# Low halves of the output weights made on GpSimd instead of VectorE, in a two-layer gated cross-attention block

## The chip, the cores and the metric

The kernel runs on one NeuronCore of a Trainium2 chip. The metric is the device time of one execution in microseconds (us). The core has five instruction queues that run side by side and wait for each other by semaphores: TensorE (PE; its weight loads are listed apart as PEld), VectorE (DVE), ScalarE (ACT), GpSimd (POOL) and SyncE (SP), which here issues every DMA. Each engine takes its own queue strictly in order.

## The reference

The input `x` is (4, 512, 512), the context (4, 512, 256), all float32. Four sub-layers are added to `x` one after another, each behind a tanh gate:

```
x = x + tanh(g_xattn[0]) * mamba(context, layernorm(x))      # conv, selective scan over 512 steps, 16 states
x = x + tanh(g_ffn[0])   * bitnet(layernorm(x))              # ternary weights, 8-bit activations
x = x + tanh(g_xattn[1]) * attention(layernorm(x), context)  # 16 heads of 128, RMS-normed q and k
x = x + tanh(g_ffn[1])   * experts(layernorm(x))             # 4 experts, 512 wide
```

What the change touches is the last product of the attention:

```
out = einsum('bhqk,bkhd->bqhd', attn, v).reshape(B, Sq, H * D)
return out @ Wo                                              # Wo is (16 * 128, 512)
```

## The kernel before

**Two halves for one float32.** Matmuls run in float16. A float32 matrix `w` is scaled by a power of two `S` and kept as a high half `hi = fp16(w * S)` and a low half `lo = fp16(w * S - hi)`; a product then takes three matmuls (`mm3`, line 252). The helper `split` (lines 241 to 244) makes the halves: ScalarE writes `hi` (L243), VectorE writes `lo` in one instruction (L244, `w * S - hi`). Everything that is split goes through these two lines, so the profile shows them under many names: `qT`, `oT`, `hlwk`, `hlwq`, `hlwo` and others.

**Staging of the attention weights.** The 16 heads form four groups (hg 0 to 3). For each group, `attention_weights` takes Wk, Wq and Wo in turn (units named `wk0`, `wq0`, `wo0`, `wk1`, ...). `raw_load` (L265) brings 128x2048 float32 of raw weights to SBUF (for k half of that), `staging` (L276) squares its pieces of 128x512 on ScalarE (L289) to find `S` (a matmul with ones at L228, then a short chain on VectorE and GpSimd, L215 to L221), splits them piece by piece, and stores both halves to DRAM (L298). Four pieces make one unit of Wo. The attention of all four batches later reads these halves back head by head (`wk` L850, `wq` L916, `wo` L1021). The raw tile and the tile of halves both come from the pool `big`, which has three buffers; the next units and the ternary weights of the bitnet layer of batches 1 and up (`w`, loaded at L715) take the same three buffers. A unit must be finished before its buffers go to the next.

**Where this happens.** Group 0 is staged in the prologue. Groups 1 to 3 are staged as filler work during the attention of batch 0: at every softmax, `filler` advances the generator by four pieces. At the same time `layer0(1)` runs, first the scan of batch 1. So in this stretch three streams share the engines: the attention heads of batch 0, the scan of batch 1, and the staging.

**The scan.** For each of 16 states and each 128-channel tile t, one step (L646 to L664) loads a row of B and a row of C broadcast to all partitions (`bc` L646, `cc` L648, five buffers together), ScalarE makes `dA` in PSUM (L652), GpSimd makes `h = du * bc` (L186), VectorE scans `dA = dA * state + h` (L659 or L662) and multiplies by `cc` (L660; for every fourth step GpSimd does it, again under L186), and TensorE transposes and sums the result into `py` (L627). The tile of `h` comes from six buffers that are shared with other tiles.

**A head of the attention.** TensorE makes scores `ps`, VectorE their row maximum (L951), ScalarE the exponentials `pr` (L971), then the halves `hl` of the probabilities: for the heads up to number 8 of a batch GpSimd (L991) and ScalarE (L989) write the high ones and VectorE the low ones (L992); for the heads from 9 on in batches 0 to 2, one of each two is made on GpSimd alone, which first scales `pr` in place (L984) and then subtracts the high half (L986). `hl` goes through a transposing DMA (L994) to `pT`. After four heads, `project` (L1028) multiplies by Wo.

**The order of the instructions.** The program order is written out by hand (heads in a loop, the scan and the fillers between them at fixed rates), but the final order on each engine is set by a list scheduler that runs over the whole program with its own estimate of every instruction's length. An edit in one place can therefore change the order of instructions that the edit does not mention, on every engine.

Of the kernel before, what the change touches and what calls it, by code (L numbers as in the profile page):

```python
# [35 lines left out]
ALU = mybir.AluOpType  # L36
# [55 lines left out]
SC = 4  # L92
PT = 3
MT = 0
AV = 4
VB = 2
WB = 5
# [13 lines left out]
def flamingo_kernel(  # L111
# [8 lines left out]
    nc = tc.nc  # L120
# [29 lines left out]
    def bigt(shape, dtype, name):  # L150
        return big.tile(shape, dtype, tag="big", name=name)
# [7 lines left out]
    def sm(n, tag, name, bufs=4):  # L159
        return small.tile([P, n], F32, tag=tag, name=name, bufs=bufs)  # L160
# [63 lines left out]
    def total_pow2(tot, pool, name):  # L224

        n = tot.shape[1]
        ps = ap(f"frobps{name}") if pool is None else psum(pool, f"frobps{name}")
        nc.tensor.matmul(ps[:, :n], ones, tot, start=True, stop=True)  # L228
        if n == 1:
            return pow2(ps[:, 0:1], name)  # L230
        s = sm(1, "ftot", f"ftot{name}")
        nc.vector.tensor_reduce(s, ps[:, :n], AX.X, ALU.add)
        return pow2(s, name)
# [4 lines left out]
        nc.scalar.activation(junk, w, AF.Square, accum_out=tot)  # L238
        return total_pow2(tot, pool, name)

    def split(w, hi, lo, S):

        nc.scalar.activation(hi, w, AF.Copy, scale=S)  # L243
        nc.vector.scalar_tensor_tensor(lo, w, S, hi, ALU.mult, ALU.subtract)  # L244

    def mm3(ps, pairs, first=True, last=True):

# [11 lines left out]
    def raw_load(name, src, tile=bigt, parts=1):  # L259

        n, m = src.shape[1] // parts, src.shape[2]
        pieces = []
        for i in range(parts):
            raw = tile([P, n * m], F32, f"raw{name}{i}")
            nc.sync.dma_start(raw.rearrange("p (a b) -> p a b", a=n), src[:, i * n : (i + 1) * n])  # L265
            pieces += [raw[:, j : j + 512] for j in range(0, n * m, 512)]
        return pieces
# [8 lines left out]
    def staging(name, src, n, ps_pool, raw=None, store=True):  # L276

        if raw is None:
            raw = raw_load(name, src)
        w = 512 * len(raw)  # L280
        hl = bigt([P, 2 * w], F16, f"hl{name}")
        v = hl.rearrange("p (n s m) -> p n s m", n=n, s=2)
        pieces = [
            (r, *(v[:, j, s] if n > 1 else v[:, 0, s, j * 512 : (j + 1) * 512] for s in range(2)))
            for j, r in enumerate(raw)
        ]
        tot = sm(4, "stot", f"stot{name}", 2)
        for j, (r, hi, lo) in enumerate(pieces):
            nc.scalar.activation(hi, r, AF.Square, accum_out=tot[:, j : j + 1])  # L289
            yield  # L290
        S = total_pow2(tot[:, : len(pieces)], ps_pool, name)
        for r, hi, lo in pieces:
            split(r, hi, lo, S[:, 1:2])
            yield
        if not store:
            return None, S, hl
        d = dram.tile([P, 2 * w], F16, name=f"d{name}")
        nc.sync.dma_start(d, hl)  # L298
        return d, S, hl

    def attention_weights(hgs, ps_pool):

        units = [(hg, w) for hg in hgs for w in "kqo"]

        def load(hg, w):
            cols = slice(hg * 512, (hg + 1) * 512)
            return raw_load(f"w{w}{hg}", {
                "k": Wk[:, cols].rearrange("(k p) c -> p k c", p=P),
                "q": Wq[hg],
                "o": Wo[cols, :].rearrange("(h p) f -> p h f", p=P),  # L310
            }[w])

        kept = {"k": (wk_d, Sk), "q": (wq_d, Sq), "o": (wo_d, So)}
        raws = [load(*units[0])]
        for j, (hg, w) in enumerate(units):
            raws += [load(*u) for u in units[j + 1 : j + 2]]
            d, S, _ = yield from staging(f"w{w}{hg}", None, 1 if w == "k" else HG, ps_pool, raws[j])
            kept[w][0].append(d)
            kept[w][1].append(S)
            if w == "q":  # L320

                c = const.tile([P, 1], F32, name=f"ceq{hg}")
                nc.vector.tensor_scalar(c, S[:, 1:2], XS * QS * (HD * EPS) ** 0.5, None, ALU.mult)
                nc.vector.tensor_tensor(c, c, c, ALU.mult)
                nc.vector.tensor_tensor(c, c, gfac, ALU.mult)
                ceq.append(c)
# [4 lines left out]
    def values_of(b, hg, wv, ps_tile, v_tile):  # L331

        for c in range(T):
            rows = slice(c * P, (c + 1) * P)
            ps = ps_tile(f"pw{b}{hg}{c}")
            mm3(ps, [(cT[b][:, 0, k, rows], cT[b][:, 1, k, rows], wv[:, 0, k], wv[:, 1, k]) for k in range(2)])
            v = v_tile([P, 2, 512], F16, f"v{b}{hg}{c}")
            split(ps, v[:, 0], v[:, 1], QS)
            yield v

    def first_values(pool, ps_tile):


        for hg in range(NG):
            raw = bigt([P, 2, 512], F32, f"rawv{hg}")
            nc.sync.dma_start(raw, Wv[:, hg * 512 : (hg + 1) * 512].rearrange("(k p) c -> p k c", p=P))
            wv = pool.tile([P, 2, 2, 512], F16, tag="wv", name=f"wv{hg}", bufs=2)
            S = frobenius(raw, wv[:, 0], psv, f"wv{hg}")
            split(raw, wv[:, 0], wv[:, 1], S[:, 1:2])
            Sv.append(S)  # L350
            wv_d.append(dram.tile([P, 2048], F16, name=f"dwv{hg}"))
            nc.sync.dma_start(wv_d[hg], wv.rearrange("p s k c -> p (s k c)"))
            for b in range(PRE):
                for c, v in enumerate(
                    values_of(b, hg, wv, ps_tile, lambda s, d, n: pool.tile(s, d, tag="v", name=f"o{n}", bufs=VB))
                ):
                    nc.sync.dma_start(v_d[b][hg][:, c, :], v.rearrange("p s c -> p (s c)"))
                    yield
# [456 lines left out]
    def split_normed(xr, stats, hl, cols, name, tag="q", xn_tag="v"):  # L815


        xn = normed(xr, stats, name, xn_tag)
        xs = midt([P, 2, L], F16, f"xs{name}", tag)
        (nc.vector.tensor_copy if name[0] in XSD else nc.scalar.copy)(xs[:, 0], xn)  # L820
        nc.gpsimd.tensor_tensor(xs[:, 1], xn, xs[:, 0], ALU.subtract)
        nc.sync.dma_start_transpose(
            hl[:, :, :, cols].rearrange("p s k r -> p (s k) r"), xs.rearrange("p s f -> p (s f)")
        )

    def attention(b):
# [70 lines left out]
        def values(hg):  # L897
            def v_tile(shape, dtype, name):
                return at.tile(shape, dtype, tag="v", name=name, bufs=AV)

# [191 lines left out]
    def stage_expert(t, i):  # L1092

        j = 3 * t + i
        if j == 0:
            expert_raw(0)
        expert_raw(j + 1)
        e_d[t, i], e_S[t, i], hl = yield from staging(f"e{t}{i}", None, 1, pss, e_raw.pop(j), t < T - 1)
        hl = hl.rearrange("p (s k c) -> p s k c", s=2, k=T)
        if t == T - 1:  # L1100
            kept.append((hl[:, 0], hl[:, 1]))
        return hl[:, 0], hl[:, 1]
# [68 lines left out]
    def last_experts(pool, places):  # L1171
# [12 lines left out]
        for t in (T - 1, *range(T - 1)):  # L1184
            xTs[t] = pool.tile([P, 2, T, P], F16, tag="v", name=f"lxT{t}", bufs=AV)
            split_normed(x_sb[b][:, t, :], estats[b][t], xTs[t], slice(0, P), f"l{t}", "q")
# [22 lines left out]
    with tc.tile_pool(name="pro", bufs=1) as pro, tc.tile_pool(name="psp", bufs=4, space=PSUM) as psp:  # L1209
# [8 lines left out]

        if MT:
            wider["t"] = pro, MT  # L1220

# [79 lines left out]
    for i in range(-2, n):  # L1301
# [14 lines left out]
        w = steps[i // NH](i % NH, 2) if i >= 0 else iter(())  # L1316
# [98 lines left out]
```

## Time and profile before

| | |
|---|---|
| median of 3 runs | 2021.76 us (2015.58 to 2025.78) |
| the profiled execution | 2021.89 us |
| its span, first to last instruction | 2020.1 us |
| instructions | 27201 |
| mean granted TensorE clock | 0.879 |

The profile is one execution. For each engine it gives the busy time of every group of instructions (line, engine, operation, output <- inputs, shape), the mean length of one in ns, and the idle time just before them with what ended it ("who waited for whom"). A view by stretches gives the busy time of each engine between two moments, which tells what limits that stretch. A timeline lists the instructions in order of time, like ones merged. Busy times over a stretch of many engines don't add up: the stretch lasts as long as the engine or the chain that binds it.

### The profile page before, as it was taken

To read this page: it belongs to the slowest core of one execution; us is meant where nothing else is said; L and a number is where in the kernel's file an instruction comes from. 1 tells how busy PE (TensorE), PEld (TensorE's weight loads), DVE (VectorE), ACT (ScalarE), POOL (GpSimd) and SP (SyncE) were. 2 spreads that over 40 slices of the span, in tenths; PEclk is the share of its full clock that TensorE was granted. 3 is DMA by queue.
4 is the path that set the end of the run, shared out by engine and by line. 5 is a ranking of instruction groups with operands and counts; after the bars stand their busy time and mean duration, and the time that the engine had idled before them with its cause. 6 is when DMAs were issued, how large, how long until landed. Compare 5 with 4: busy or idle time off the path is not lost. (4 is left out here: it accounts for less than half of the span.)

```text
span 2020.1 us, 27201 instructions
## 1 busy us (share of the span) xinstructions
PE 1634.6 (81%) x8366; PEld 899.8 (45%) x8366; DVE 1541.3 (76%) x2893; ACT 1333.7 (66%) x3123; POOL 941.3 (47%) x931
## 2 busy tenths in 40 slices
PE   4364698657789987778999878798999879798888
PEld 1343233344444444455444554454444445455456
DVE  5899776999998778799886984999764565654664
ACT  6787656756666876475658665666565775857673
POOL 1886311785754269385414783675133441413211
PEclk8555798767789998989999899898999889898999
DMA  7454557778775587766435887676445686767655
GB/s 269 171 166 136 161 156 229 183 223 218 219 207 130 129 216 176 210 165 164 99 87 148 192 201 190 157 183 142 96 84 131 131 212 172 205 163 181 185 138 152
DMA packets 516322, 342.50 MB, mean 170 GB/s; under 512 B 425800, under 2 KB 427976, under 8 KB 510032
## 3 DMA queue, kind: packets, MB, share of 16 engines
q1 hardware_dynamic: 516176, 340.77, 64.9%
q8 instruction: 65, 1.06, 0.2%
q14 instruction: 81, 0.66, 0.1%
HBM read 193.10 MB, written 44.30 MB: 118 GB/s over the span
## 5 line engine op out<-in xcount | busy, mean ns | idle before, releaser
L186 POOL TENSOR_TENSOR h<-u,bc 128x512 f32<-128x512 f32 x256 | 338.2, 1341 | 86.4 <-DMA bc<-bd 43.7
L627 PE MATMUL py<-ident,h 128*128 128x128 f32 x1024 | 196.4, 337 | 123.9 <-DVE h L660 95.4
L652 ACT ACTIVATE dA<-delta,A 128x512 f32<-128x512 f32 x256 | 172.4, 685 | 140.5 <-DVE h L660 105.1
L252 PE MATMUL ps<-kT,qT 128*128 128x512 f16 x768 | 213.2, 399 | 50.1 <-ACT pr L971 34.4
L252 PE MATMUL pav<-pT,v 128*128 128x256 f16 x1536 | 215.6, 296 | 42.9 <-DMA pT<-hl 19.3
L659 DVE TENSOR_TENSOR_SCAN dA<-dA,h 128x512 f32<-128x512 f32 x200 | 240.7, 1217 | 11.4 <-POOL h L186 6.6
L627 PEld LDWEIGHTS py<-ident,h 128*128 128x128 f32 x1024 | 164.3, 213 | 166.7 <-DVE h L660 122.8
L951 DVE TENSOR_REDUCE nmx<-ps 128x1 f32<-128x512 f32 x256 | 172.4, 680 | 69.1 <-PE ps L252 68.8
L252 PE MATMUL pq<-axnT,wq 128*128 128x512 f16 x768 | 206.2, 423 | 19.9 <-DVE ksq L880 7.8
L992 DVE SCALAR_TENSOR_TENSOR hl<-pr,den,hl 128x512 f16<-128x512 f32 x214 | 193.7, 923 | 32.6 <-ACT hl L989 18.3
L971 ACT ACTIVATE pr<-ps,nmx,rqs 128x512 f32<-128x512 f32 x256 | 197.7, 775 | 14.2 <-DVE hl L992 10.1
L252 PEld LDWEIGHTS <-v 128*128 128x128 f16 x1536 | 161.5, 106 | 99.6 <-issue 33.8
L252 PE MATMUL pwo<-wo,oT 128*128 128x512 f16 x768 | 178.7, 383 | 9.0 <-DVE oT L244 5.5
L991 POOL TENSOR_SCALAR hl<-pr,den 128x512 f16<-128x512 f32 x86 | 63.6, 740 | 237.9 <-issue 104.6
L252 PEld LDWEIGHTS <-wq 128*128 128x128 f16 x768 | 83.1, 109 | 130.1 <-issue 64.6
L183 POOL TENSOR_TENSOR rqs<-ssq,mhalf 128x4 f32<-128x4 f32 x64 | 68.7, 1073 | 148.7 <-ACT ssq L940 140.9
L660 DVE TENSOR_TENSOR h<-dA,cc 128x512 f32<-128x512 f32 x200 | 134.3, 679 | 4.4 <-DMA cc<-bd 0.7
L252 PEld LDWEIGHTS <-qT 128*128 128x128 f16 x768 | 76.2, 102 | 137.0 <-issue 65.2
L252 PEld LDWEIGHTS <-cT 128*128 128x128 f16 x768 | 79.0, 105 | 113.3 <-issue 45.0
L252 PEld LDWEIGHTS <-oT 128*128 128x128 f16 x768 | 74.7, 99 | 99.8 <-DVE oT L244 8.4
L989 ACT ACTIVATE hl<-pr,den 128x512 f16<-128x512 f32 x128 | 91.8, 717 | 36.4 <-DVE den L978 30.0
L252 PE MATMUL pk<-wk,cT 128*128 128x512 f16 x384 | 106.4, 420 | 11.3 <-ACT ssq L940 6.2
(387 smaller groups left out, 3481.5 us busy)
## 6 DMA issues: line engine op xcount, KB each, us to landing
bc<-bd SPq DMA_DIRECT2D x112, 256.0 KB, 4.2
cc<-bd SPq DMA_DIRECT2D x112, 256.0 KB, 3.9
wq<-dwq SPq DMA_DIRECT2D x64, 256.0 KB, 4.4
wo<-dwo SPq DMA_DIRECT2D x64, 256.0 KB, 3.5
w<-w3d SPq DMA_DIRECT2D x12, 1024.0 KB, 7.0
de<-hle SPq DMA_DIRECT2D x9, 1024.0 KB, 5.5
lw<-de SPq DMA_DIRECT2D x18, 512.0 KB, 4.9
wk<-dwk SPq DMA_DIRECT2D x16, 512.0 KB, 3.5
```

The source lines that it names most:

```text
L183: nc.gpsimd.tensor_tensor(res, arg, mhalf[:, : arg.shape[1]], ALU.pow)
L186: nc.gpsimd.tensor_tensor(out, a, b, ALU.mult)
L252: nc.tensor.matmul(ps, l, r, start=first and i == 0, stop=last and i == n - 1)
L627: nc.tensor.matmul(ys[g // gs][:, g % gs, t, :], src[:, g::T], ident, is_transpose=True, start=first and t == 0 and g % gs == 0, stop=last ...
L652: last = nc.scalar.activation(dA, delta[t0 + t], AF.Exp, scale=A[:, t0 + t, n : n + 1])
L659: nc.vector.tensor_tensor_scan(dA, dA, h, 0.0, ALU.mult, ALU.add)
L660: nc.vector.tensor_tensor(h, dA, cc, ALU.mult)
L951: nc.vector.tensor_reduce(nmx[:, c : c + 1], ps, AX.X, ALU.max, negate=True)
L971: mark[0] = nc.scalar.activation(pr, scs[c], AF.Exp, bias=nmx[:, one], scale=rqs[:, one], accum_out=den[:, c - c0 : c - c0 + 1],).ins
L989: nc.scalar.activation(hl[:, c, 0], prs[c], AF.Copy, scale=den[:, one])
L991: nc.gpsimd.tensor_scalar(hl[:, c, 0], prs[c], den[:, one], 1.0, ALU.mult, ALU.mult)
L992: nc.vector.scalar_tensor_tensor(hl[:, c, 1], prs[c], den[:, one], hl[:, c, 0], ALU.mult, ALU.subtract)
```

## The change

For the units `wo1`, `wo2` and `wo3`, `split` no longer makes the low half on VectorE with one instruction. GpSimd makes it with two: the first scales the raw piece in place (`w = w * S`), the second subtracts the high half (`lo = w - hi`). The scaling overwrites the raw piece, so it has to wait until ScalarE has read it for `hi`. The three units have 12 pieces of 128x512 together. `wo0` and everything else that is split stays as it was. The line numbers of the changed kernel are higher by 1 from line 95, and by 5 behind `split`.

```diff
+STAGE_POOL = ("wo1", "wo2", "wo3")
...
-    def split(w, hi, lo, S):
+    def split(w, hi, lo, S, by_pool=False):
 
         nc.scalar.activation(hi, w, AF.Copy, scale=S)
-        nc.vector.scalar_tensor_tensor(lo, w, S, hi, ALU.mult, ALU.subtract)
+        if by_pool:
+            nc.gpsimd.tensor_scalar(w, w, S, 1.0, ALU.mult, ALU.mult)
+            nc.gpsimd.tensor_tensor(lo, w, hi, ALU.subtract)
+        else:
+            nc.vector.scalar_tensor_tensor(lo, w, S, hi, ALU.mult, ALU.subtract)
...
         for r, hi, lo in pieces:
-            split(r, hi, lo, S[:, 1:2])
+            split(r, hi, lo, S[:, 1:2], name in STAGE_POOL)
```

## Prediction

> **What bounds the kernel now.** I read the page first. Over the whole span no engine is full, so the average says little about a change that lives in one stretch:
>
> ```profile
> PE 1634.6 (81%) x8366; PEld 899.8 (45%) x8366; DVE 1541.3 (76%) x2893; ACT 1333.7 (66%) x3123; POOL 941.3 (47%) x931
> ```
>
> The view by tile says where the change lives: the instructions that write `hlwo` run from 218 to 592 us, four for `wo0` (kept) and twelve for `wo1` to `wo3`.
>
> ```profile
> L244 DVE SCALAR_TENSOR_TENSOR hlwo<-rawwo,Swo,hlwo x16: 734/750/1748, 230.6 to 592.3; 128x512 f16<-128x512 f32 x16
> ```
>
> The columns are min/median/max in ns. The wide maximum matters below. So I asked for the busy time by stretches around it (us in the stretch, then PE, PEld, DVE, ACT, POOL):
>
> ```profile
> 400.00:450.00 50.00, 31.49 (x149) 22.65 (x150) 48.74 (x66) 29.98 (x76) 38.31 (x32) 0.66 0.78 212
> 450.00:500.00 50.00, 33.44 (x173) 21.37 (x173) 46.13 (x75) 31.67 (x67) 29.39 (x25) 0.76 0.84 232
> 500.00:550.00 50.00, 37.84 (x185) 23.45 (x183) 46.84 (x71) 30.53 (x77) 35.59 (x30) 0.81 0.68 207
> 550.00:600.00 50.00, 40.40 (x227) 25.04 (x226) 47.45 (x95) 38.69 (x104) 28.00 (x28) 0.88 0.79 199
> 600.00:650.00 50.00, 49.23 (x244) 22.44 (x241) 42.09 (x118) 31.27 (x84) 21.36 (x33) 1.00 0.67 166
> ```
>
> From 400 to 600 us VectorE is busy for 92 to 97% and everything else has air; from 600 us TensorE takes over (98%). So twelve instructions are taken off the engine that binds. The timeline shows what one unit costs today:
>
> ```profile
> 422.39 4.48 DVE L244 SCALAR_TENSOR_TENSOR hlwo<-rawwo,Swo,hlwo 128x512 f16<-128x512 f32 x3
> 426.80 2.33 DVE L659 TENSOR_TENSOR_SCAN dA<-dA,h 128x512 f32<-128x512 f32 x2
> ```
>
> and the waits between 404 and 438 us show who stood still meanwhile (total, times, longest):
>
> ```profile
> ACT dA L652 <- DVE h L660: 12.8, 6, 6.6
> PE py L627 <- DVE h L660: 11.6, 4, 7.2
> ```
>
> **What goes.** The same stretches for `hlwo` alone give VectorE 5.87 us for `wo1` (404 to 438), 4.91 for `wo2` (499 to 527) and 2.80 for `wo3` (580 to 600): 13.58 us.
>
> **What comes.** GpSimd already does this pair of operations on this shape for the probabilities:
>
> ```profile
> L986 POOL TENSOR_TENSOR hl<-pr,hl 128x512 f16<-128x512 f32 x42 | 51.5, 1226 | 27.1 <-ACT hl L985 27.1
> L984 POOL TENSOR_SCALAR pr<-pr,den 128x512 f32<-128x512 f32 x42 | 32.1, 765 | 48.4 <-DVE den L978 47.2 <-DMA hqT<-hq 0.7 <-DVE qmx L700 0.2
> ```
>
> So a unit costs GpSimd 4 x 0.765 + 4 x 1.226 = 7.96 us, three units 23.9 us. GpSimd has room for that on average, but its queue feeds the scan, and each burst stands in it in front of `h` products. Busy in the three stretches:
>
> ```profile
> 404.00:438.00 34.00, 17.09 (x82) 13.00 (x81) 33.09 (x44) 16.29 (x36) 26.05 (x22) 0.60 0.78 215
> 499.00:527.00 28.00, 22.05 (x112) 14.47 (x111) 24.84 (x32) 15.28 (x31) 17.90 (x15) 0.83 0.69 227
> 580.00:600.00 20.00, 17.41 (x100) 10.36 (x100) 18.77 (x51) 13.69 (x32) 7.40 (x9) 0.91 0.75 204
> ```
>
> *Unit wo1.* The diff alone doesn't tell the new order, so I compared the order the scheduler writes for both programs. In the changed one, GpSimd gets between the last `h` of scan step 8 and the last of step 12: the 8 new instructions, 8 products `h` (1.341 each), 3 products with `cc` (1.292) and one `ks` (1.218), in all 7.96 + 10.73 + 3.88 + 1.22 = 23.8 us. VectorE gets, up to the scan that reads this last `h`, a run of scan work with nothing else in it: 9 scans (1.217) and 7 products (0.679), 15.7 us. Matching products to scans one by one in the timeline, GpSimd had finished step 8 at 419.2 us, and VectorE would come to step 8 at 426.8 - 5.9 = 420.9 us. The last `h` of step 12 is then ready at 443.0, and VectorE wants it at 436.6: it waits 6.4 us, with the attention's instructions queued behind the waiting scan and TensorE and the score buffers behind these. Without the burst it would be ready at 435.0. So of `wo1`'s 5.9 us nothing is left: +0.5 (between -5.9, if TensorE or the loads hold the scan back so that GpSimd gets ahead, and +2.1, the whole burst against what is removed). I take +0.5.
>
> *Unit wo2.* Here the order puts row maxima, `oT` and four updates of x (L1028) between the scans. From the end of the L991 ahead of the burst GpSimd needs 4 x 0.765 + 3 x 1.226 + 5 x 1.341 = 13.4 us to the last `h` of step 5, VectorE 14.0 us to its scan. No wait: -4.9. If the stretch stood by itself it couldn't be shorter than GpSimd's 17.90 + 7.96 = 25.9 us, which would leave -2.1 of the 28. I take -4.9 and keep -2.1.
>
> *Unit wo3.* The scan is over; the burst is one block, and behind it in the queue stand the row statistics `rstf` of bitnet 1, which today start at 589.2 us after 3.2 us of idle. They open the way to bitnet's first matmul (613.9 us). VectorE gains up to 2.8; bitnet can lose up to 7.96 - 3.2 = 4.8. I take 0. The unit's buffers go on to bitnet's weights `w`: the load that today follows the store at 596.4 us is first needed at 615.8 us, so 5 us later costs nothing.
>
> *Shared access.* `hlwo` takes 734 ns or up to 1748. Matched against the GpSimd rows, the like L992 takes 0.744 us where no two-input GpSimd instruction overlaps it (118 cases) and 1.167 where one does (89); the scans, which read PSUM, take 1.217 either way. Between 350 and 590 us 60 VectorE instructions of this kind remain, one in 4.0 us; 12 new subtractions of 1.226 are each met by 1.98 / 4.0 of one, 5.9 meetings x 0.42 = 2.5 us. For `wo1` VectorE waits anyway, so I charge two thirds: +1.7 (0 to 5.9 x 1.19 = 7.0, with the longest L992, 1.935).
>
> By the Trainium skill, "SBUF — State Buffer", section "Who interferes with whom", the loser of such a meeting blocks fully until the other is done. On average half a subtraction would be left, 0.61 us per meeting by that rule in place of 0.42, and the sum would be 0.7 us higher. The rule agrees with which rows are slow, and the mean is the trace's. Against the whole change speaks "GPSIMD Engine Reference", "Engine selection": elementwise work with two inputs belongs on VectorE, GpSimd being about twice as slow. The rows say 1.99 us against 0.75, even worse; but the rule prices the engines, and the stretches say which one binds.
>
> *Queues and order.* SP's own waits show it standing 5.2 us in front of a store of `hlwo` today. In the new order the `wo1` store stands seven places later, behind the loads of step 12 and of the first row of step 13, and waits for GpSimd; if GpSimd is late, the rows of steps 13 and 14 are late with it. That is inside the +2.1 above. The squares of `wk2` need a buffer of `wo1`, and its sum moves behind about three more scan steps; the keys that need it come about 12 steps later, so no cost. Then, the scheduler writes another order for all engines from 420 to about 1550 us, with no more work there; the last 535 VectorE instructions are as before. The trace can't price that: the longest single waits are about 7 us, one won or lost in each of the two later rounds of scan and bitnet is -14 to +14. I take 0.
>
> **Sum.** +0.5 - 4.9 + 0 + 1.7 = -2.7 on the profiled execution's 2021.9 us (span 2020.1 and 1.8 around it), which is the median (2021.8): about **2019**.
>
> **Rivals.** Faster or slower below means by over 0.5%, 10 us, about what a measurement of this kernel can tell.
>
> *All of it is kept:* GpSimd is idle for 79 of the 240 us from 350 to 590, and other streams on VectorE fill the gaps: -13.6 + 1.7 = -11.9, 2010. For it: 97% on VectorE. Against it: the lead of `h` over its scan is 5.2 us in the median, less than a burst. It decides where VectorE has other work between the scans, as in `wo2`. 0.30, with a lucky order.
>
> *GpSimd becomes the bound, slower:* at every unit the burst goes through in full to the scan and to `rstf`, 23.9 - 13.6 + 2.5 = +12.8, 2035. It decides as soon as the lead is used up before the burst begins, as worked out for `wo1`. Against it: the four long idles of GpSimd around `wo2`. 0.20.
>
> *The new order costs more than the change is worth:* +14 in the later rounds, 2033. 0.08.
>
> That the change doesn't do what it says is out: the new order has 24 more instructions on GpSimd and 12 fewer on VectorE.
>
> **Numbers.** Forecast within 0.5%: 0.42, own range 2012 to 2031. Faster 0.30, slower 0.28. The 8-in-10 range reaches to both sides: 2004 to 2036.
>
> **What will show it.** Right: 12 fewer L244 on VectorE and the two new GpSimd groups near 0.77 and 1.2 us; VectorE idle for some 6 us on GpSimd's `h` after `wo1`, and none in `wo2`; bitnet 1 starting within 5 us of 613.9 less the gain; L992 a little longer between 400 and 600. Wrong: no such idle (then nearer 2010), or long `h` waits at all units, or stretches after 700 us that change by over 7 us each.

## The result, and the profile after

The changed kernel takes 2039.51 us (median of 7 runs, 2035.66 to 2056.86) against 2025.85 us for the kernel before (7 runs, 2015.58 to 2030.15): a ratio of 1.010, 95% interval 1.0077 to 1.0123. The interval is 16 to 25 us; the two medians differ by only 13.7 us (a ratio of 1.007), so the size of the loss is less sure than its sign. The forecast was 2019. The profiled execution took 2035.66 us with a span of 2033.9 and is the fastest of its seven.

The work did what the forecast said of it. Page, busy time by engine over the span of the changed kernel:

```profile
PE 1631.4 (80%) x8366; PEld 895.3 (44%) x8366; DVE 1526.3 (75%) x2881; ACT 1335.2 (66%) x3123; POOL 958.2 (47%) x955
```

VectorE has 12 instructions and 15.0 us less (1541.3 before), GpSimd 24 instructions and 16.9 us more (941.3 before). The view of the tile `rawwo` in the changed kernel gives the pair's lengths (min/median/max in ns):

```profile
L246 POOL TENSOR_SCALAR rawwo<-rawwo,Swo x12: 687/692/1122, 414.5 to 585.0; 128x512 f32<-128x512 f32 x12
L247 POOL TENSOR_TENSOR hlwo<-rawwo,hlwo x12: 1147/1166/1596, 421.1 to 587.0; 128x512 f16<-128x512 f32 x12
...
L249 DVE SCALAR_TENSOR_TENSOR hlwo<-rawwo,Swo,hlwo x4: 741/745/752, 228.8 to 231.3; 128x512 f16<-128x512 f32 x4
```

The means are 742 and 1211 ns; 765 and 1226 were forecast. The same stretches as before, in the changed kernel (us in the stretch, then PE, PEld, DVE, ACT, POOL, then the granted clock, the DMA share and GB/s):

```profile
400.00:450.00 50.00, 26.23 (x123) 18.41 (x122) 43.44 (x58) 28.11 (x65) 48.33 (x42) 0.69 0.73 193
450.00:500.00 50.00, 39.29 (x189) 23.09 (x188) 46.95 (x79) 34.14 (x78) 29.79 (x28) 0.77 0.90 242
500.00:550.00 50.00, 37.96 (x212) 24.37 (x211) 44.71 (x71) 34.00 (x89) 38.42 (x34) 0.86 0.74 226
550.00:600.00 50.00, 38.14 (x205) 23.17 (x203) 45.03 (x90) 31.71 (x87) 30.63 (x33) 0.90 0.78 212
600.00:650.00 50.00, 44.77 (x217) 20.45 (x215) 38.53 (x108) 32.26 (x86) 20.80 (x33) 0.97 0.67 123
```

From 400 to 450 us VectorE falls from 48.74 to 43.44, and GpSimd, at 48.33 of 50, is the engine that binds. The waits of the changed kernel between 404 and 438 us (total, times, longest) show who now stands behind it:

```profile
ACT dA L657 <- DVE h L665: 16.6, 8, 3.7
...
PE py L632 <- POOL h L187: 13.3, 2, 9.5
...
DVE dA L664 <- POOL h L187: 4.1, 5, 1.6
```

VectorE waits for GpSimd's `h`, as was worked out for `wo1`: 4.1 us here and 6.3 between 400 and 600, in several short waits and not in one of 6.4; before, it waited for `h` at none of these places. In `wo2` it waits 1.0 us for `h` between 490 and 540, so nearly nothing, as forecast. Bitnet of batch 1 has its first matmul at 616.3 us (613.9 before, within 5 us as forecast). All of this is near the forecast.

The loss comes later. The table sets the start of the same instruction (its end in the rows that say "ends", and in the last row) in several kernels beside the kernel before, in us, each read from the trace of one profiled execution. Executions of one kernel differ by 10 us and more: A's is the fastest of its 7, D's of its 12, and G's the slowest but one of its 11. Columns: A the changed kernel; B old work in the new order; C new work in the old order; D, E, F new work with the new order only until 646, from 646 to 1265, and from 1265 us; G old work in a third order, told of at the end.

| event | before | A | B | C | D | E | F | G |
|---|---|---|---|---|---|---|---|---|
| scan of batch 1, step 8 | 426.8 | -10.4 | -6.6 | -5.0 | -8.8 | -6.5 | -7.8 | +1.1 |
| scan of batch 1 ends | 574.9 | -0.6 | +5.7 | +4.4 | +1.7 | +2.2 | +0.8 | +3.4 |
| bitnet of batch 1 ends | 746.3 | +2.2 | +7.0 | +5.7 | +4.2 | +3.8 | +2.1 | +4.2 |
| scan of batch 2 ends | 953.2 | +14.7 | +21.5 | +7.4 | +1.0 | +15.9 | +0.1 | +7.4 |
| bitnet of batch 2 starts | 974.8 | +23.7 | +31.7 | +7.4 | +1.0 | +25.2 | +0.3 | +21.1 |
| bitnet of batch 2 ends | 1128.1 | +12.5 | +19.2 | +7.2 | -1.4 | +13.9 | 0.0 | -0.8 |
| head 8 of batch 2 | 1417.1 | +23.2 | +29.4 | +8.1 | -0.4 | +13.3 | +16.7 | +6.0 |
| bitnet of batch 3 ends | 1524.7 | -7.9 | -1.7 | +7.7 | -1.2 | +12.2 | -14.4 | -17.5 |
| first head of batch 3 | 1594.1 | +13.4 | +18.2 | +7.8 | +0.3 | +12.2 | +6.8 | -5.5 |
| last update of x | 1981.7 | +13.7 | +18.9 | +7.7 | -2.6 | +11.6 | +7.7 | -4.1 |

Column A is within 2.2 us of before at 746 us, when all the moved work has long been done. Then layer 0 of batch 2 runs up to 24 us late, the heads of batch 2 end up 23 us late, and bitnet of batch 3 is 8 us early. No work differs there; only the order does.

### The profile page after: what moved, and what is told of

Its sections match the earlier page's. It is cut to its first block, busy times and chain, and to the rows that moved or that the text cites. A ratio compares the mean times of both kernels' runs of the same rounds, so it can differ in the third digit from the quotient of the medians.

```text
span 2033.9 us, 27185 instructions
## 1 busy us (share of the span) xinstructions
PE 1631.4 (80%) x8366; PEld 895.3 (44%) x8366; DVE 1526.3 (75%) x2881; ACT 1335.2 (66%) x3123; POOL 958.2 (47%) x955
## 5 line engine op out<-in xcount | busy, mean ns | idle before, releaser
L632 PE MATMUL py<-ident,h 128*128 128x128 f32 x1024 | 202.4, 344 | 134.1 <-DVE h L665 95.9
L257 PE MATMUL pav<-pT,v 128*128 128x256 f16 x1536 | 203.8, 285 | 46.8 <-DMA pT<-hl 28.9
L257 PE MATMUL pq<-axnT,wq 128*128 128x512 f16 x768 | 197.2, 409 | 20.2 <-ACT ssq L945 5.1
L997 DVE SCALAR_TENSOR_TENSOR hl<-pr,den,hl 128x512 f16<-128x512 f32 x214 | 185.6, 884 | 34.7 <-ACT hl L994 17.4
L257 PEld LDWEIGHTS <-v 128*128 128x128 f16 x1536 | 155.3, 102 | 99.6 <-issue 42.2
L257 PE MATMUL pwo<-wo,oT 128*128 128x512 f16 x768 | 183.0, 388 | 5.4 <-DVE oT L249 2.5
L257 PE MATMUL pk<-wk,cT 128*128 128x512 f16 x384 | 113.9, 443 | 18.1 <-DMA wk<-dwk 11.2
```

The costliest lines, as they stand in the source:

```text
L257: nc.tensor.matmul(ps, l, r, start=first and i == 0, stop=last and i == n - 1)
L632: nc.tensor.matmul(ys[g // gs][:, g % gs, t, :], src[:, g::T], ident, is_transpose=True, start=first and t == 0 and g % gs == 0, stop=last ...
L997: nc.vector.scalar_tensor_tensor(hl[:, c, 1], prs[c], den[:, one], hl[:, c, 0], ALU.mult, ALU.subtract)
```

## The experiments

Two theories stood against each other. *Order*: the loss comes from the new order that the scheduler wrote for all engines. *Work*: GpSimd's 24 us hold up the scan. To part them, an order can be written out: the instructions of each engine are listed, and each is tied to the one ahead of it by an edge that orders without adding a semaphore (`PIN` holds one list for each engine). The scheduler then has no choice left.

```diff
+def pin(tc, nc):
+    traced = {i.name: i for i in nc.cur_bb.bb.instructions}
+    for text in PIN:
+        ids = pinned_order(text)
+        for a, b in zip(ids, ids[1:]):
+            tc.add_manual_dep(
+                traced[f"I-{b}"], f"I-{a}",
+                mybir.DependencyInfo(mybir.DependencyClass.NoSync, mybir.DependencyReason.DATA), reason="pin",
+            )
...
         flamingo_kernel(tc, *args, res)
+        pin(tc, nc)
```

Ratios are to runs of the kernel before on the same chip, with a 95% interval. The kernel before has a wide spread itself: 29 runs beside the first four experiments lay between 2010.65 and 2030.63 us. A single profiled execution can therefore be 10 us off its kernel's median, so the ratios decide, and the traces show only places. The kernel before was not run with its own order written out. Three results below speak against a large price of the writing out itself: written-out orders took 1.0095 and 0.9942 where the scheduler's own kernels with the same order and other work took 1.010 and 0.9949, and the order of before with four pieces moved took 1.0006.

### Work and order apart

**New work, old order.** The changed kernel with the order of before on every engine; each GpSimd pair stands where the VectorE instruction stood.

> The 24 GpSimd instructions of the change, in the order of before: on every engine the instructions stand as in the kernel before, and each pair of new ones stands where the VectorE instruction stood that it replaces. Theory 'order' (the loss is made by the new order of all engines after 600 us, the moved work itself is nearly free): a ratio to before between 0.993 and 1.003, nearest 0.999, the 2.7 us of the predicted sum. Theory 'work' (GpSimd's 24 us hold up the scan, and what follows is only passed on): 1.007 to 1.012, like the change itself, with waits of VectorE on GpSimd's h of over 15 us between 400 and 600 us.

Measured: 2030.25 us, 1.0026 (1.0006 to 1.0045). VectorE's waits for `h` between 400 and 600 us come to 11.8 us, less than the 15 that *work* asked for. **Old work, new order.** The kernel before, with the twelve instructions on VectorE, in the order of the changed kernel.

> The twelve VectorE instructions of before, in the order of the changed kernel: each stands where the subtraction on GpSimd stood in the scheduler's list, all others as in the changed kernel. Theory 'order': a ratio of 1.007 to 1.013, the whole loss without the change, with the scan and bitnet of batch 2 late by 10 to 20 us as in the changed kernel. Theory 'work': 0.997 to 1.003.

Measured: 2041.26 us, 1.0095 (1.0065 to 1.0126). The scan and bitnet of batch 2 are late by 21.5 and 31.7 us (column B), more than expected. The order alone makes a loss as large as the whole, and the work alone about a quarter of it: *work* falls. In the table, column C shows the same thing from the other side. It is 5.7 us late at 746 us, and from there on, where its order is that of before, it stays between 7.2 and 8.1 us late (7.7 at the end). Column A runs 4 to 8 us ahead of B all the way from step 8, so in the order written for it the moved work gained about 5 us in the traces; the medians (2039.51 and 2041.26, from different chips) show less, and the ratios (1.010 and 1.0095) nothing.

### One unit at a time

Here the scheduler was free, so each kernel has its own order as well as its own work.

```diff
-STAGE_POOL = ("wo1", "wo2", "wo3")
+STAGE_POOL = ("wo1",)
```

> The change for the unit wo1 alone, with the order that the scheduler then writes. Theory 'work': a third of the loss, about 1.003 (the burst that the prediction priced at +0.5 us net), and more than for wo3 alone, where no scan is running. Theory 'order': the moved work explains nothing, the three single units differ from each other by more than their thirds would, anywhere from 0.995 to 1.015.

Measured for `wo1` alone: 2027.16 us, 1.0031 (1.0009 to 1.0053).

> The change for the unit wo3 alone, with the order that the scheduler then writes. Theory 'work': within 2 us of before (0.999 to 1.001), as the scan of batch 1 is over when its burst runs. Theory 'order': anywhere from 0.995 to 1.015, and not in line with its share of the moved work.

Measured for `wo3` alone: 2028.89 us, 1.0021 (1.0000 to 1.0042), although no scan runs beside `wo3`. These two runs don't part the theories: 1.0031 is what *work* expected of `wo1`, and the interval of `wo3` reaches down into its 0.999 to 1.001. `wo2` alone was not run in an order of its own. Bitnet of batch 2 starts 23.2 us late with `wo1` alone and has ended 8.5 us late, and the profiled execution ends 1.0 us late: a stream can slip by 20 us and get most of it back. Column G has the same: bitnet of batch 2 starts 21.1 us late there, and the kernel has the lowest ratio of all. So a late stream is no loss in itself.

### Where the order loses

The two orders differ from about 420 to 1560 us, but at any moment only about a hundred instructions at most are on different sides. So one order can be left for the other at a cut: at 646 and 1265 us, where fewer than ten differ. All three kernels have all of the moved work.

> All of the moved work, with the changed kernel's order up to about 646 us (the end of wo3) and the order of before from there on. With the order of before throughout the same work took 1.0026 of the time of before, with the new order throughout 1.010. Theory 'middle' (the loss is made between 646 and 1265 us, where layer 0 of the second round runs 15 to 25 us late) and theory 'last' (it is made between 1265 and 1560 us): 0.996 to 1.003, since the 5 us that the scheduler's own place for the moved work gains up to step 8 of the second scan stay. Theory 'spread' (each stretch adds a part): 1.002 to 1.007. That the streams drift apart already in front of 646 us: 1.007 to 1.012.

Measured: 2029.55 us, 1.0033 (1.0015 to 1.0051). Its profiled execution (column D) was the fastest of its 12, so column D ends too early.

> All of the moved work, in the order of before except between about 646 and 1265 us, where the order is the changed kernel's. Theory 'middle': 1.007 to 1.013, with the second bitnet starting 10 to 25 us later than in the run with the order of before throughout. Theory 'last': 1.000 to 1.005. Theory 'spread': 1.004 to 1.007.

Measured: 2033.40 us, 1.0057 (1.0036 to 1.0078).

> All of the moved work, in the order of before up to about 1265 us and in the changed kernel's from there on. Theory 'middle': 1.000 to 1.005. Theory 'last' (the heads of the third batch fall behind there while bitnet 3 ends early): 1.007 to 1.012. Theory 'spread': 1.004 to 1.007.

Measured: 2034.94 us, 1.0050 (1.0029 to 1.0071). Against 1.0026 for the old order throughout, the three stretches add 0.0007, 0.0031 and 0.0024; with the 1.0026 that makes 1.0088, and the changed kernel has 1.010. *Spread* fits all three ratios; *middle* and *last* fit only towards the ends of the intervals. So the two later stretches most likely both lose. The intervals are as wide as the single terms, so this and the split between the two are not shown beyond doubt.

What a lost stretch looks like is seen from 866 to 960 us, the scan of batch 2, which ends 8.5 us later in column E than in column C. First new work in the old order, then the kernel with the new order from 646 to 1265 us:

```profile
866.00:960.00 94.00, 77.83 (x418) 49.48 (x419) 91.61 (x123) 63.47 (x162) 70.38 (x59) 0.89 0.68 167
```

```profile
866.00:960.00 94.00, 77.82 (x403) 48.16 (x402) 85.13 (x119) 59.70 (x149) 67.06 (x56) 0.88 0.67 170
```

VectorE, which binds here at 91.61 of 94 us, falls to 85.13. Its waits from 845 to 960 us in the second kernel, and then in the first:

```profile
DVE bstz L192 <- DMA x<-in_x: 6.1, 1, 6.1
DVE xnz L621 <- ACT zth L620: 4.0, 2, 3.5
DVE dA L664 <- ACT dA L657: 2.6, 2, 1.4
DVE dA L664 <- POOL h L187: 1.9, 1, 1.9
```

```profile
DVE bstz L192 <- DMA x<-in_x: 4.5, 1, 4.5
DVE qT L249 <- ACT qT L244: 1.9, 1, 1.9
...
DVE xnz L621 <- ACT zth L620: 1.2, 2, 0.8
```

All of its waits there come to 18.7 us against 10.7. The longest is only 1.6 us longer; the rest are small waits on several producers. No single wait carries the loss.

### The block of GpSimd work in front of `h`

`wo2` was the unit from which the forecast took a real gain. Here it moves alone, in the old order, each pair at the VectorE instruction's place.

> Only the unit wo2 moves to GpSimd, each GpSimd pair where the VectorE instruction stood, every other instruction in the order of before. The working of the forecast (-4.9 for wo2, and about +0.6 for shared access): 4 us less than before, 0.998. Theory 'the burst stands in front of the products h' (as in the run with all the work in the old order, which lost 5 us): 1.000 to 1.003, with VectorE waiting over 2 us on h between 499 and 530 us.

Measured: 2024.44 us, 1.0006 (0.9986 to 1.0027). No gain, and the timeline shows where it went:

```profile
510.05 1.15 POOL L247 TENSOR_TENSOR hlwo<-rawwo,hlwo 128x512 f16<-128x512 f32 x1
511.16 3.71 POOL L187 TENSOR_TENSOR h<-u,bc 128x512 f32<-128x512 f32 x3
512.45 1.22 DVE L667 TENSOR_TENSOR_SCAN h<-dA,h 128x512 f32<-128x512 f32 x1 [5.37 <-POOL h L187]
```

The four pairs stand in one block, the products `h` behind it start at 511.16 us, and the scan has waited 5.37 us: the 4.9 us that left VectorE, and a little more. So the same work was put into two gaps in which GpSimd idles before, two pairs from 509.7 us and two from 517.9 us of the kernel before (in the new run they start at 506.5 and 515.0 us), with nothing else moved but the unit's store and the next unit's load, which follow it.

> The unit wo2 alone on GpSimd and every other instruction in the order of before, as in the run with wo2 in the old order (1.0006), but the four GpSimd pairs stand in two gaps in which GpSimd idles before (from 509.7 us, 3.5 us long, and from 517.9 us, 4.0 us long) and not in one block in front of the products h; the store and the next unit's load follow the last pair. Theory 'place' (the block made VectorE wait 5.4 us for h, which ate the 4.9 us): that wait is below 1.5 us, the second scan ends 3 to 6 us earlier than with the block, and the time is 0.996 to 0.999. Theory 'the gain is lost later anyway': the second scan ends earlier, the time is 0.9995 to 1.002.

Measured: 2024.55 us, 1.0020 (0.9999 to 1.0042). VectorE's waits between 490 and 540 us, first with the block and then with the gaps:

```profile
DVE h L667 <- POOL h L187: 5.4, 1, 5.4
DVE nmx L956 <- PE ps L257: 2.8, 1, 2.8
```

```profile
DVE nmx L956 <- PE ps L257: 6.1, 1, 6.1
DVE dA L664 <- POOL h L187: 1.9, 1, 1.9
```

The scan no longer waits 5.4 us for `h`, but the row maximum now waits 6.1 for the scores instead of 2.8 (3.1 in the kernel before), and `h` still costs 1.9, over the 1.5 that *place* allowed. VectorE is busy 39.98 of those 50 us, 40.38 with the block. The scan of batch 1 ends only 0.6 us earlier than with the block, where *place* expected 3 to 6. So the theory that the place of the block costs the gain falls, in the time and in the trace: what went from the wait for `h` came back as a wait for the next producer.

### Is any new order worse?

To see other orders with next to no work moved, only the last of the four pieces of one unit went to GpSimd: one VectorE instruction less, one pair more.

```diff
-            split(r, hi, lo, S[:, 1:2], name in STAGE_POOL)
+            split(r, hi, lo, S[:, 1:2], name == STAGE_POOL and r is pieces[-1][0])
```

> Of the twelve pieces only the last one of wo1 moves: one VectorE instruction of about 0.75 us (1.4 at most) less, one GpSimd pair of about 1.9 us more, the scheduler's own order. The moved work by itself: -1.4 to +1.2 us, 0.999 to 1.001. The new order differs from that of before in 4010 of TensorE's instructions, as many as with all twelve pieces. Theory 'any new order' (before has an order that happens to fit the chip well, and most other orders that the scheduler writes are worse by some us in the later rounds): 1.002 to 1.012, with the loss behind 600 us. Theory 'this order' (only the changed kernel's order is bad): 0.998 to 1.002.

> Only the last piece of wo2 moves; the order is the scheduler's own and differs in 3841 of TensorE's instructions. The moved work by itself: 0.999 to 1.001. Theory 'any new order': 1.002 to 1.012 in at least two of the three runs with one piece. Theory 'this order': 0.998 to 1.002.

> Only the last piece of wo3 moves; the order is the scheduler's own and differs in 3742 of TensorE's instructions. The moved work by itself: 0.999 to 1.001. Theory 'any new order': 1.002 to 1.012 in at least two of the three runs with one piece. Theory 'this order': 0.998 to 1.002.

Measured: 2025.65 us, 1.0013 (0.9994 to 1.0033); 2022.77 us, 0.9996 (0.9974 to 1.0018); 2010.71 us, 0.9949 (0.9930 to 0.9968). The theory that any new order is worse falls, since at most one of the three is slower, and so does the one that only the changed kernel's order departs from before: a rewritten order is worth something of either sign. The last one gains about 10 us from an edit that moves 2 us of work. Two more kernels asked whether that gain belongs to the order, and what all twelve pieces cost in it.

> All work as before (nothing moves to GpSimd), in the order that the scheduler wrote for the run with one piece of wo3 moved (0.9949); the piece's VectorE instruction stands where its GpSimd pair stood. Theory 'order, of either sign' (the time follows the order and hardly the work that was moved): 0.993 to 0.998. Theory 'the work that left VectorE at the end of wo3 opened the way to bitnet' (the gain comes from the piece): 0.999 to 1.002.

Measured: 2014.79 us, 0.9942 (0.9924 to 0.9961).

> All twelve pieces on GpSimd, each pair where the VectorE instruction stood, in the order that the scheduler wrote for the run with one piece of wo3 moved. Theory 'order, of either sign', with the work's price from the run in the order of before (1.0026): 0.995 to 1.001, so about 0.3% above the run with the old work in this order. Theory 'the moved work makes the loss in any order but that of before': above 1.003. Theory 'in another order the moved work gains what was forecast or more': below 0.994.

Measured: 2017.84 us, 0.9971 (0.9949 to 0.9993). Both are where the theory of the order put them. Work and order stand apart in both pinned pairs: the twelve pieces cost 1.0026 in the old order and 0.9971 / 0.9942 = 1.0029 in this one, while the order makes 0.9942, 1 or 1.0095 with the same work. The kernel before in this third order has the lowest ratio of all, though not clear of the 0.9949, and moves nothing.

## Why the prediction was wrong, by its steps

- **What is removed and what comes.** Right: twelve instructions fewer on VectorE, pairs of 742 and 1211 ns on GpSimd.
- **`wo1`, +0.5.** The mechanism was right, a wait for `h` that takes back most of what VectorE gave (5.9 us): 4.1 us between 404 and 438 us in the changed kernel, 5.3 there with the new work in the old order, for 6.4 forecast. That the waits from 400 to 600 us sum to 6.3 is chance, as they hold `wo2`'s too.
- **`wo2`, -4.9.** In the changed kernel's order the wait is 1.0 us, as forecast. That the gain reaches the end is not shown: with `wo2` alone in the old order nothing was left (1.0006), and without the block's wait nothing either (1.0020).
- **`wo3`, 0.** Bitnet of batch 1 started within 2.4 us of before. That fits; the unit's work was not measured by itself in the old order.
- **Shared access, +1.7.** It doesn't show: the instructions of L992 took 1019 ns in the mean between 350 and 590 us, and 1021 before. But 2.5 us over 60 instructions would be 42 ns each, and the three kernels with GpSimd work in the order of before scatter from 989 to 1036, so a price of this size isn't excluded.
- **The sum of the work, -2.7.** With the pairs at VectorE's places the work costs +0.26% and +0.29%, some 5 to 6 us, so for these places the sum was about 8 us too low. In the changed kernel's own order it isn't decided: the ratios, 1.010 and 1.0095, put the work at +1 us, the traces at about -5, and the intervals hold both. Either way the work is too little to account for the result.
- **"The new order", 0 between -14 and +14.** This is the step that failed. The order alone makes 1.0095, 19 us. The bound came from "one won or lost in each of the two later rounds" at 7 us for the longest single wait. The runs showed another thing: a loss that is most likely spread over two stretches of about 600 and 300 us; and in the part of the first that is shown above (845 to 960 us) no wait of VectorE grew by over 3 us, but several grew, by 8.0 us together. The longest wait of a profile is no bound for what a rewritten order can do. The rival that named the order had the right sign and place with 0.08 of the chance and 14 us; its size was too small, and its chance too. Nothing here shows that the sign could have been read from the trace before: six orders that the scheduler wrote for variants of this one edit took 0.9949 to 1.010 of the time.
- **What would show it wrong.** "Stretches after 700 us that change by over 7 us each" is what happened: +12.5 us from 746 to 953 us, and +10.7 from 1128 to 1417.

Open is why one arrangement of the same instructions fits better than another. The traces show where time is lost, as many small waits, and the experiments show that it is the order; none of them says what in the third order, G, makes it good.

## What to carry to other kernels

Where a scheduler writes the order, an edit has two prices: its work, and the order that comes with it. Here the second was 19 us, and the first lay between a gain of about 5 and a loss of about 6, and nothing in the diff told of the second; pin the order and time the two apart before judging an idea. A forecast for such a kernel should give the order a spread of its own, here -0.6% to +1.0%, in place of a single wait. Work that leaves the engine that binds is worth little if the next producer is as late: with `wo2`, VectorE's freed 5 us became a wait for GpSimd, and with that gone a wait for TensorE.

## What the runs showed of the hardware

The granted clock (the share of TensorE's full speed that the profile shows as granted) moved with the order. Averaged over all runs of a kernel it was 0.881 for the kernel before (22 runs, 0.875 to 0.886), 0.888 for the same work in the third order (11 runs beside them on the same chip, 0.886 to 0.891), 0.877 for the changed kernel (7 runs) and 0.875 for old work in its order (6 runs, beside 29 of the kernel before at 0.880). In the third order TensorE's page row is

```profile
PE 1621.4 (80%) x8366; PEld 890.3 (44%) x8366; DVE 1543.4 (77%) x2893; ACT 1337.0 (66%) x3123; POOL 944.0 (47%) x931
```

for the same 8366 matmuls that took 1634.6 us before. TensorE idles 394.6 us of its span of 2016.0, more than the 385.5 before, and is still done earlier, because the matmuls are 13.2 us shorter. In the changed kernel the busy time is 3.2 us shorter and the idle time 17.0 longer. So in these two executions the third order saves in the matmuls and not in idle time. That the higher clock makes its gain is likely from this, but no run varied the clock by itself. By stretches, 750 to 980 us in the kernel before, the changed kernel and the third order (the clock is third from the end):

```profile
750.00:980.00 230.00, 180.33 (x946) 110.32 (x944) 204.05 (x341) 141.99 (x361) 155.83 (x144) 0.90 0.68 172
```

```profile
750.00:980.00 230.00, 180.50 (x966) 112.56 (x964) 194.89 (x300) 138.81 (x346) 150.79 (x134) 0.88 0.69 173
```

```profile
750.00:980.00 230.00, 180.45 (x1016) 113.35 (x1013) 206.42 (x326) 150.26 (x386) 161.46 (x145) 0.93 0.78 182
```

Busy within 0.2 us of each other, TensorE gets through 946, 966 and 1016 matmuls. The counts don't follow the clock alone (966 go with the lowest), as the stretches don't hold the same matmuls: `pav` has 192, 216 and 216 of them, `ps` 104, 102 and 117. Whether the order sets the clock directly or through the gaps that it leaves, these runs don't settle. From 350 to 2000 us TensorE has 9 idle gaps of over 3.4 us in the kernel before, 12 in the third order and 21 in the changed one.

The Trainium skill, "TensorE: Matmul & The Clock Gate", section "What's actually happening", says that an idle window of about 3.4 us halves the clock and a busy one restores it. The count of the changed kernel agrees with its lower clock, that of the third order does not agree with its higher one, and new work in the third order and old work in the changed kernel's have 17 such gaps each, at clocks of 0.887 and 0.873 in these executions. So such a count doesn't foretell the clock in this case.
